# Moving the last normalisation of a fused attention layer from VectorE to GpSimd, with earlier weight splits and new scheduling keys

## The chip, the cores and the metric

The kernel runs on one core of one Trainium2 chip. The metric is device microseconds of one execution; the median of several runs is given. A profiled execution gives, beside its own time, the span from the first to the last instruction and every engine's work in it.

Short names are used throughout: PE is TensorE (the matrix engine), PEld its weight loads, DVE is VectorE, ACT is ScalarE, POOL is GpSimd, SP is SyncE, whose queue issues the DMA transfers (SPq in the profile).

## The reference

The input x has 4 batches of 512 rows and 256 columns. Each row is normalised, then two branches are computed from the normalised rows and multiplied, and x is added.

```
xn = layernorm(x)
# attention branch: 16 query heads of 128, 4 key/value groups, causal
Q, K, V = xn@Wq + bq, xn@Wk + bk, xn@Wv + bv
attn = softmax(Q K^T / sqrt(128) + causal mask)
y = gelu((attn V) @ Wo + bo)              # exact gelu
r = xn + y                                # the outer residual
s = (r - mean(r)) * rsqrt(var(r) + 1e-5) * gamma + beta
# gate branch
g = silu((silu(xn@Wgate) * (xn@Wup)) @ Wdown)   # 256 -> 1024 -> 256
out = x + s * g
```

The kernel rewrites the last two lines as out = (r - mean) * rstd * (g * gamma) + (g * beta + x).

## The kernel before

**Tiling.** Rows are handled in tiles of 128, so a batch has four tiles t = 0..3. The attention of a batch runs in four phases, one for each key/value group g, which four heads share; the 16 phases are numbered ph = 4b + g. All products in TensorE use values split in two parts (a high part rounded to the multiplier's precision and the low rest), and each product is three matmuls: high by high, high by low, low by high.

**Before the ordered part.** The first stretch of the program normalises x, transposes it, and computes the gate branch of the first three batches (`gate_up`, `down`). In its loop over b and f, `split_group` splits the query and output weights of groups 1 to 3 into two parts on POOL, using the probability tiles p1 and p2 as room, and writes the parts to device memory (`w_dram_q`, `w_dram_o`); later phases reload them. The first group is split separately. At the end of this stretch `clear` sets the edges of the probability tiles to zero (MEMSET at L273), so the edges of p1 and p2 wait until the last split's writes have landed. The multiplier, gate and shift parts g * gamma and g * beta + x go to device memory together with xn, as `fin_dram`. This stretch is ordered by the framework's scheduler.

**The ordered part.** From `order = Order(tc, nc)` on, the kernel lists tasks with an engine, an estimated cost, a key and the tasks that must come first. `Order.run` is a list scheduler that plays these through at build time: whenever an engine comes free it takes the ready task with the lowest key. The result is a fixed order of instructions on each engine; on the chip each engine runs its own list in that order, and an instruction that waits holds all behind it on its engine. `KEYS` holds 30 numbers that go into the keys, and so shape that order. The recording helper makes all of these instructions appear as L49 in the profile; they are told apart by the names of their tiles. A task's `lag` is the planner's estimate of the time from its end until others can use the result; for the loads of `fin` it is 4.0.

**A phase.** Its tasks and tile names:
- Q*, K*, V*: products for queries (into `bank`), keys (`pk`) and, once per batch, values (`pv`), then their split by ACT (high) and DVE (low) into `qT`, `kT` and `v`. `Kw` (`k0`) on POOL joins the first 128 keys again for the first scores. Values go through device memory and come back as `vr`.
- Sp, M, E, R, N: for each row tile i and subtile t the scores (`ps`, two buffers, shared with `pk` and `pv`), the mask and row minimum on DVE (`p<-ps,mask`, `least`), the exponential with its sum on ACT, the inverse of the sum on DVE, and the normalising on POOL (`p<-p,total`).
- T, H, L: transposed blocks (`u`, DVE), their high part (`pT`, ACT) and low part (`pT<-u,pT`, POOL, 1.3 us each, ten in a phase).
- W: weighted sums of values with `pT`, into the four `bank`s; then Ch and Cl (`ctxT`, ACT and DVE) and Y, the output product, into `py`.

**The outer residual.** After the fourth phase of a batch O adds the bias (DVE), G applies gelu (ACT), and for each tile: F loads `fin` (xn, g * gamma, g * beta + x) into one of two `gate` buffers, F0 adds xn (`residual`, POOL), F1 takes mean and variance (`moments2`, DVE), F2 the inverse root (`root2`, POOL), F3 `gated` and F4 `gated2` finish the tile in two DVE instructions with two tensor inputs each:

```
y = (y - mean) * fin[1]        # F3, DVE, needs F1
y = y * rstd + fin[2]          # F4, DVE, needs F2 and F3; frees the gate buffer
```

F5 stores the tile. For the first three batches this runs beside the next batch's phases; for the last it is the end of the program.

Of the kernel before, what the change touches and what calls it, by code (L numbers as in the profile page):

```python
# [14 lines left out]
ALU = mybir.AluOpType  # L15
# [4 lines left out]
EPS = 1e-5  # L20
S = 32
MASK = -1e9
KEYS = {"q0": 1.13, "q1": -0.213, "k": 1.41, "v0": 2.413, "v1": -1.03, "s0": -2.626, "s1": 0.729, "s2": -0.184, "n": -5.431, "t0": -5.662, "t1": 6.581, "t2": 4.665, "h": 0.821, "l": -0.262, "w0": -1.18, "w1": -0.794, "c": 4.145, "y0": 0.4, "y1": 1.301, "f0": 4.654, "f1": 6.182, "wo": 29.85, "wq": 0.68, "vr": 3.1, "ls": 1.3, "lt": -16.956, "lc": 5.897, "lw": 2.853, "da": 3.184, "db": 0.216}
RUNS = ((0, 1), (2, 3))
ON_ACT = (0, 1)
HIGHEST = 3.4028235e38
# [133 lines left out]
def kernel(  # L160
# [39 lines left out]
    pe, dve, act, pool, sp = nc.tensor, nc.vector, nc.scalar, nc.gpsimd, nc.sync  # L200
    latest = {}

    @contextmanager
    def behind(*keys):

        with ExitStack() as stack:
            for k in keys:
                for ins in latest[k]:
                    stack.enter_context(tc.issue_after(ins.ins))
            yield  # L210
# [23 lines left out]
    mhalf = const.tile([P, NT], F32, name="mhalf")  # L234
# [6 lines left out]
    def split_sbuf(dst, src, hi_on, lo_on):  # L241
        if hi_on is nc.scalar:
            nc.scalar.copy(dst[0], src)
        else:
            hi_on.tensor_scalar(dst[0], src, 1.0, 1.0, ALU.mult, ALU.mult)
        lo_on.tensor_tensor(dst[1], src, dst[0].bitcast(F32), ALU.subtract)
# [74 lines left out]
    rstd = const.tile([P, B, NT], F32, name="rstd")  # L321
# [33 lines left out]
    def transposed(b, t):  # L355

        if t == 0:
            xT[b] = [pair("pt", 4, f"xT_{b}_{c}") for c in range(ND)]
        xn = [normed(b, t), normed(b, t + 1)]
        pt = psum.tile([P, ND, 2, P], F32, tag="s", bufs=2, name=f"pxt_{b}_{t}")  # L360
        for c in range(ND):
            for k in range(2):
                nc.tensor.transpose(pt[:, c, k], xn[k][:, ts(c, P)], ident)
        for c in range(ND):
            dst = xT[b][c][:, :, ds(t * P, 2 * P)]
            latest["xT"] = split_psum(dst, pt[:, c].rearrange("p k q -> p (k q)"))
        if t + 2 == NT:
            for c in range(ND):
                nc.sync.dma_start(xT_dram[b][:, c], xT[b][c].bitcast(F32))

    def reload(b):
        xT[b] = [pair("xT", 2, f"xT_{b}_{c}_again") for c in range(ND)]
        for c in range(ND):
            nc.sync.dma_start(xT[b][c].bitcast(F32), xT_dram[b][:, c])
# [140 lines left out]
    def gate_up(b, f):  # L515
        gate_up_product(b, f)
        gate_silu(b, f)
        gate_times_up(b, f)
        inner_hi(b, f)
        inner_lo(b, f)  # L520
# [27 lines left out]
    def down(b, t):  # L548
        down_product(b, t)
        gate(b, t)  # L550
        gate_scaled(b, t, 0)
        gate_scaled(b, t, 1)
        gate_shifted(b, t)
        gate_out(b, t)
# [52 lines left out]
    q0, k0, vr, bank, turned = {}, {}, {}, {}, {}  # L607
# [222 lines left out]
    acc, ys = {}, {}  # L830
    mv2 = mv
# [21 lines left out]
    def activated(b, t0, t1):  # L853
        act.activation(ys[b][:, t0:t1], ys[b][:, t0:t1], AF.Gelu)

    fin, rs2 = {}, {}
# [12 lines left out]
        rs2[b, t] = rstd[:, b, t : t + 1]  # L869
        dve.tensor_scalar(rs2[b, t], mv2[:, b, t, 1:2], EPS, 1.0, ALU.add, ALU.mult)  # L870

    def root2(b, t):
        pool.tensor_tensor(rs2[b, t], rs2[b, t], mhalf[:, :1], ALU.pow)

    def gated(b, t):
        y, f = ys[b][:, t], fin[b, t]
# [24 lines left out]
    def split_group(kind, g):  # L901


        st = work.tile([P, 1024], F32, tag="stage", bufs=2, name=f"st_{kind}{g}")
        if kind == "q":
            for c in range(ND):
                nc.sync.dma_start(st[:, ts(c, 512)].rearrange("p (a n) -> p a n", a=G), wq_v[c, g])
        else:
            nc.sync.dma_start(st.rearrange("p (a n) -> p a n", a=G), wo_v[g])
        for k in range(2):  # L910
            flat = p_tiles[1 + k].rearrange("p a n -> p (a n)")
            hi, lo = flat[:, :512], flat[:, 512:1024]
            split_sbuf((hi.bitcast(F32R), lo.bitcast(F32R)), st[:, ts(k, 512)], nc.gpsimd, nc.gpsimd)
            nc.sync.dma_start(w_dram[kind, g][:, 0, ts(k, 512)], hi)
            nc.sync.dma_start(w_dram[kind, g][:, 1, ts(k, 512)], lo)

    def first_group(kind):
        views = [wq_v[c, 0] for c in range(ND)] if kind == "q" else [wo_v[0]]
        w = load_w(f"{kind}0", views)
        nc.sync.dma_start(w_dram[kind, 0], w.bitcast(F32))  # L920
        return w

    wqs[0] = first_group("q")
    wos[0] = first_group("o")

    for b in range(B - 1):
        for f in range(NI):
            gate_up(b, f)
            if b and f in (4, 5, 6):

                with behind("shifted"):
                    split_group(*(("q", 1), ("o", 1), ("q", 2), ("o", 2), ("q", 3), ("o", 3))[3 * b + f - 7])
            if b > 0 and f < NT:
                down(b - 1, f)
            if b + 1 < B:
                if f in (3, 5):
                    transposed(b + 1, f - 3)
                if b + 2 == B and f == NI - 1:
                    reload(0)
# [6 lines left out]
    pe, dve, act, pool, sp = (order.engine(e) for e in (nc.tensor, nc.vector, nc.scalar, nc.gpsimd, nc.sync))  # L946
    NPH = B * KV
    for name, n in (("s", 2), ("u", 4), ("ctx", 3), ("gate", 2), ("stage", 1)):
        order.ring(name, n)
    K = KEYS  # L950
    weights, done_w = {}, {}

    def add(name, engine, cost, key, emit, args, **kw):
        order.task((name, *args), engine, cost, key, lambda: emit(*args), **kw)
# [4 lines left out]
    def group_of(ph):  # L959
        return divmod(ph, KV)  # L960
# [8 lines left out]
    for f in range(NI):  # L969
        b, key = B - 1, -8.0 + 0.1 * f  # L970
# [8 lines left out]
    for b in (B - 2, B - 1):  # L979
        e = "POOL" if b + 1 < B else "DVE"  # L980
        c = 0.75 if b + 1 < B else 0.85
# [11 lines left out]
        for t in range(NT):  # L993
            key = base + K["db"] * t + K["da"]
            after = [("Dx", b, t), ("Da", b, t // 2), ("gb",)]
# [8 lines left out]
    for ph in range(NPH):  # L1004
        b, g = group_of(ph)
# [98 lines left out]
        for m, run in enumerate(runs):  # L1104
# [3 lines left out]
            else:  # L1108
# [8 lines left out]
                after=deps, mode=1,  # L1117
# [20 lines left out]
        if g == KV - 1:  # L1138
            late = b == B - 1
            key = ph + 1.5 + K["f0"]  # L1140
            if late:
                for t in range(NT):
                    done = [("O", b, t)] + [("E", b, g, i, u) for i, u in tiles]
                    add("G", "ACT", 0.35, key + 0.1 * t, lambda b, t: activated(b, t, t + 1), (b, t), after=done, mode=3)
            else:
                order.task(("G", b), "ACT", 3.6, key, lambda b=b: activated(b, 0, NT), after=[("O", b, t) for t in range(NT)], mode=3)
            for t in range(NT):
                k = key + (0.1 if late else K["f1"]) * t
                if late and t > 1:
                    done = [("Qp", b, g, r) for r in range(G)] + [("Kp", b, g)] + [("Vp", b, t) for t in range(NT)]  # L1150
                    add("F", "SP", 0.4, ph, load_fin, (b, t), after=done, lag=4.0)
                else:
                    done = [("O", b, 0)] if not late else [("F5", b - 1, t) for t in range(NT)]
                    add("F", "SP", 0.4, ph if late else k - 0.5, load_fin, (b, t), takes="gate", after=done, lag=4.0)
                add("F0", "POOL", 0.76, k, residual, (b, t), after=[("F", b, t), ("G", b, t) if late else ("G", b)])
                add("F1", "DVE", 0.6, k, moments2, (b, t), after=[("F0", b, t)])
                add("F2", "POOL", 0.65, k, root2, (b, t), after=[("F1", b, t)])
                add("F3", "DVE", 1.1, k, gated, (b, t), after=[("F1", b, t)])
                add("F4", "DVE", 1.1, k, gated2, (b, t), after=[("F2", b, t), ("F3", b, t)], gives=(("gate", "F", b, t),))
                add("F5", "SP", 0.4, k, stored, (b, t), after=[("F4", b, t)])  # L1160

    def idle_work(k):
# [60 lines left out]
```

## Time and profile before

| | us |
|---|---|
| median of 3 runs | 645.4 (643.51 to 647.47) |
| the profiled execution | 649.52 |
| its span | 647.7 |
| PE busy | 621.4 (96% of the span) |
| DVE busy | 433.6 (67%) |
| ACT busy | 405.7 (63%) |
| POOL busy | 444.7 (69%) |
| granted PE clock, mean over the span | 0.981 |

In the profile's rows a group reads: line, engine, operation, output<-inputs by tile names, shapes, count, busy time and mean of one, and the idle time ahead of it with what ended it. In a timeline a row begins with its start and its duration in us, xN is the number of instructions joined in it, and the square bracket gives how long the engine stood idle before it and what released it. In the windows the columns are named where they are shown.

Weighted products (W) of the batches' first groups start at 182.2, 307.2, 425.2 and 548.3 us, which places the batches in time; the last of all starts at 626.5.

### The profile page before, as it was taken

Reading aid. Unit: us, or ns where it says so; the run is one execution under the profiler, and the core shown is the slowest. Engines: PE = TensorE matmul, PEld = TensorE weight load, DVE = VectorE, ACT = ScalarE, POOL = GpSimd, SP = SyncE. Lnnn points to the kernel's source line nnn. Section 1 sums busy time; section 2 is a strip of 40 time slices with the busy share of each in tenths; the row PEclk is TensorE's granted clock in tenths of the full one; section 3 lists DMA queues with packets and bytes.
Section 4 is the critical chain, followed back from the end, with each engine's and each line's share of the span. In section 5 each row is a group of like instructions: output and inputs, shape, how many; then the busy total and the mean of one; then the engine's idle time right before and its main releaser. Section 6 shows DMA issues by size and latency. Waiting matters only on the chain.

```text
span 647.7 us, 15888 instructions
## 1 busy us (share of the span) xinstructions
PE 621.4 (96%) x6004; PEld 554.6 (86%) x6004; DVE 433.6 (67%) x1143; ACT 405.7 (63%) x1025; POOL 444.7 (69%) x577
## 2 busy tenths in 40 slices
PE   7999999799999999999999999997999999999994
PEld 6888887788989899898899989976989888898894
DVE  5973636366357676588668586878777598778545
ACT  3442426375357777598649676884587598658662
POOL 4597777286316984778678694957596687779663
PEclk8999999999998999999899999997999999999998
DMA  6867769417595568725975955195857815958701
GB/s 207 273 209 249 258 230 325 127 38 184 157 282 171 141 178 204 220 75 130 294 212 139 286 166 147 50 306 130 239 203 150 232 63 169 272 168 217 154 2 35
DMA packets 86238, 118.10 MB, mean 182 GB/s; under 512 B 5648, under 2 KB 72336, under 8 KB 82064
## 3 DMA queue, kind: packets, MB, share of 16 engines
q1 hardware_dynamic: 86160, 117.08, 62.6%
q8 instruction: 47, 0.77, 0.5%
q14 instruction: 31, 0.25, 0.1%
HBM read 87.70 MB, written 29.36 MB: 181 GB/s over the span
## 4 chain that ended last, share of the span: by engine, by line
PE 76%; DMA 8%; DVE 5%; POOL 5%; SPq 2%; ACT 2%; issue 1%; POOLq 0%; DVEq 0%
PE bank L49 30%; PE ps L49 13%; PE py L49 11%; PE pv L49 3%; DMA vr<-v_dram 3%; PE pk L49 2%; DMA w_dram_o<-p 2%; PE pd L49 2%; PE bank L229 2%; PE bank L230 2%; PE bank L231 2%; POOL pT L49 2%; POOL p L49 2%; DVE p L49 1%; DVE y L49 1%
## 5 line engine op out<-in xcount | busy, mean ns | idle before, releaser
L49 ACT ACTIVATE p<-p,least 128x32 f32<-128x32 f32 (+15 forms) x256 | 131.7, 516 | 69.4 <-DVE least L49 66.8
L49 POOL TENSOR_SCALAR p<-p,total 128x384 f32<-128x384 f32 (+7 forms) x248 | 118.9, 500 | 73.9 <-DVE total L49 68.0
L49 DVE CUSTOM_DVE_ANT_0 p<-ps,mask 128x32 f32<-128x32 f32 (+15 forms) x256 | 104.5, 431 | 70.0 <-PE ps L49 69.1
L49 PE MATMUL ps<-kT,qT 128*128 128x512 f32 (+11 forms) x576 | 116.7, 334 | 7.5 <-DVE least L49 6.8
L49 POOL TENSOR_TENSOR pT<-u,pT 128x512 fp32r<-128x512 f32 x83 | 107.4, 1305 | 23.6 <-ACT pT L49 21.8
L49 PE MATMUL bank<-pT,vr 32*128 32x128 f32 (+15 forms) x3072 | 122.3, 309 | 0.7 <-DMA vr<-v_dram 0.7
L49 PEld LDWEIGHTS bank<-pT,vr 32*128 32x128 f32 x3072 | 114.1, 186 | 8.8 <-issue 2.7
L49 PE MATMUL py<-w_o,ctxT 128*128 128x256 f32 x768 | 114.4, 289 | 0.8 <-DVE ctxT L49 0.8
L49 PEld LDWEIGHTS py<-w_o,ctxT 128*128 128x128 f32 x768 | 104.9, 192 | 4.3 <-DVE ctxT L49 1.2
L49 PEld LDWEIGHTS ps<-kT,qT 128*128 128x128 f32 x576 | 88.6, 191 | 19.2 <-DVE least L49 14.5
L49 POOL TENSOR_TENSOR pT<-u_more,pT 128x512 fp32r<-128x512 f32 x77 | 99.9, 1306 | 7.1 <-ACT pT L49 6.9
L49 PE MATMUL bank<-xT_again,w_q 128*128 128x512 f32 x384 | 95.9, 400 | 4.1 <-DVE ctxT L49 3.6
L49 PEld LDWEIGHTS bank<-xT_again,w_q 128*128 128x128 f32 x384 | 72.3, 192 | 19.4 <-DVE ctxT L49 4.3
L49 DVE STREAM_TRANSPOSE u<-p 128x512 f32<-128x512 f32 x83 | 57.9, 700 | 16.0 <-POOL p L49 14.9
L49 ACT ACTIVATE ctxT<-bank,bv_sb 128x512 fp32r<-128x512 f32 x64 | 41.9, 683 | 38.4 <-PE bank L49 33.6
L49 ACT CAST pT<-u 128x512 fp32r<-128x512 f32 x83 | 50.5, 622 | 22.7 <-DVE u L49 15.2
L49 DVE STREAM_TRANSPOSE u_more<-p 128x512 f32<-128x512 f32 x77 | 53.6, 700 | 10.8 <-POOL p L49 6.8
L49 ACT CAST pT<-u_more 128x512 fp32r<-128x512 f32 x77 | 47.5, 618 | 8.3 <-DVE u_more L49 7.2
L49 DVE SCALAR_TENSOR_TENSOR ctxT<-bank,bv_sb,ctxT 128x512 fp32r<-128x512 f32 x64 | 46.6, 738 | 8.8 <-ACT ctxT L49 8.8
L49 DVE SCALAR_TENSOR_TENSOR qT<-bank,bq_sb,qT 128x384 fp32r<-128x384 f32 x64 | 38.5, 603 | 19.4 <-ACT q L49 17.8
L49 ACT ACTIVATION_READ_ACCUMULATOR p<-p,least 128x1 f32 x256 | 48.2, 188 | 0.0
L49 ACT ACTIVATE qT<-bank,bq_sb 128x384 fp32r<-128x384 f32 x64 | 37.2, 581 | 8.6 <-PE bank L49 8.4
(133 smaller groups left out, 940.8 us busy)
## 6 DMA issues: line engine op xcount, KB each, us to landing
vr<-v_dram SPq DMA_DIRECT2D x128, 256.0 KB, 7.0
w_q<-w_dram_q SPq DMA_DIRECT2D x15, 1024.0 KB, 5.3
w_o<-w_dram_o SPq DMA_DIRECT2D x15, 1024.0 KB, 10.4
v_dram<-v SPq DMA_DIRECT2D x16, 512.0 KB, 3.6
fin<-fin_dram SPq DMA_DIRECT2D x16, 384.0 KB, 7.9
xT_dram<-xT SPq DMA_DIRECT2D x8, 512.0 KB, 5.0
fin_dram<-gate SPq DMA_DIRECT2D x16, 256.0 KB, 3.5
xT_again<-xT_dram SPq DMA_DIRECT2D x8, 512.0 KB, 4.5
```

What stands on the lines that cost most here:

```text
L49: made = getattr(self.engine, name)(*args, **kw)
L229: pe.matmul(out_ap, lhs[0], rhs[0], start=first, stop=False, **kw)
L230: pe.matmul(out_ap, lhs[0], rhs[1], start=False, stop=False, **kw)
L231: pe.matmul(out_ap, lhs[1], rhs[0], start=False, stop=last, **kw)
```

## The change

Three edits.

- **The outer residual.** In batches 0 to 2, F2 takes the roots of two tiles in one instruction (after both tiles' F1). F3 becomes `normed2`, one DVE instruction with one tensor input and two per-partition scalars, and has to wait for the root. The multiplication by fin[1] (`scaled2`, task Fg) and the sum with fin[2] (`shifted2`, F4) go to POOL as two instructions. The last batch stays as it was, with other estimated costs.
- **The splits.** Which group is split at which (b, f) is now read from a table. The order of the six splits is the same; before, three came in batch 1 (f = 4, 5, 6) and three in batch 2 (f = 4, 5, 6). Now four come in batch 1 (f = 4 to 7) and two in batch 2 (f = 4, 5).
- **The keys.** All 30 numbers in `KEYS` but none of the names change, so the order of many instructions moves a little on every engine.

```diff
-KEYS = {"q0": 1.13, "q1": -0.213, "k": 1.41, "v0": 2.413, "v1": -1.03, "s0": -2.626, "s1": 0.729, ... "f0": 4.654, "f1": 6.182, ...}
+KEYS = {"q0": 1.294, "q1": -0.162, "k": 1.154, "v0": 2.242, "v1": -0.947, "s0": -2.531, "s1": 0.181, ... "f0": 1.31, "f1": 4.659, ...}
...
-    def root2(b, t):
-        pool.tensor_tensor(rs2[b, t], rs2[b, t], mhalf[:, :1], ALU.pow)
+    def root2(b, t, n=1):
+        r = rstd[:, b, t : t + n]
+        pool.tensor_tensor(r, r, mhalf[:, :n], ALU.pow)
+
+    def normed2(b, t):
+        y = ys[b][:, t]
+        dve.tensor_scalar(y, y, mv2[:, b, t, 0:1], rs2[b, t], ALU.subtract, ALU.mult)
+
+    def scaled2(b, t):
+        y = ys[b][:, t]
+        pool.tensor_tensor(y, y, fin[b, t][:, 1], ALU.mult)
+
+    def shifted2(b, t):
+        y = ys[b][:, t]
+        pool.tensor_tensor(y, y, fin.pop((b, t))[:, 2], ALU.add)
...
+    splits = {(1, 4): ("q", 1), (1, 5): ("o", 1), (1, 6): ("q", 2), (1, 7): ("o", 2), (2, 4): ("q", 3), (2, 5): ("o", 3)}
...
-            if b and f in (4, 5, 6):
+            if (b, f) in splits:
                 with behind("shifted"):
-                    split_group(*(("q", 1), ("o", 1), ("q", 2), ("o", 2), ("q", 3), ("o", 3))[3 * b + f - 7])
+                    split_group(*splits[b, f])
...
-                add("F2", "POOL", 0.65, k, root2, (b, t), after=[("F1", b, t)])
-                add("F3", "DVE", 1.1, k, gated, (b, t), after=[("F1", b, t)])
-                add("F4", "DVE", 1.1, k, gated2, (b, t), after=[("F2", b, t), ("F3", b, t)], gives=(("gate", "F", b, t),))
+                if late:
+                    add("F2", "POOL", 0.72, k, root2, (b, t), after=[("F1", b, t)])
+                    add("F3", "DVE", 0.5, k, gated, (b, t), after=[("F1", b, t)])
+                    add("F4", "DVE", 0.5, k, gated2, (b, t), after=[("F2", b, t), ("F3", b, t)], gives=(("gate", "F", b, t),))
+                else:
+                    if t % 2:
+                        add("F2", "POOL", 0.72, k, lambda b, t: root2(b, t - 1, 2), (b, t), after=[("F1", b, t - 1), ("F1", b, t)])
+                    add("F3", "DVE", 0.4, k, normed2, (b, t), after=[("F2", b, t | 1)])
+                    add("Fg", "POOL", 0.73, k, scaled2, (b, t), after=[("F3", b, t)])
+                    add("F4", "POOL", 0.73, k, shifted2, (b, t), after=[("Fg", b, t)], gives=(("gate", "F", b, t),))
```

The whole table of keys is `q0 q1 k v0 v1 s0 s1 s2 n t0 t1 t2 h l w0 w1 c y0 y1 f0 f1 wo wq vr ls lt lc lw da db`; those of one letter or of a letter and a digit set the place of the tasks above, the last ones that of the last phase and of the late part of the gate branch.

More of the change, by code (lines that the diff above doesn't have):

```diff
@@ L22 @@
 MASK = -1e9
-KEYS = {"q0": 1.13, "q1": -0.213, "k": 1.41, "v0": 2.413, "v1": -1.03, "s0": -2.626, "s1": 0.729, "s2": -0.184, "n": -5.431, "t0": -5.662, "t1": 6.581, "t2": 4.665, "h": 0.821, "l": -0.262, "w0": -1.18, "w1": -0.794, "c": 4.145, "y0": 0.4, "y1": 1.301, "f0": 4.654, "f1": 6.182, "wo": 29.85, "wq": 0.68, "vr": 3.1, "ls": 1.3, "lt": -16.956, "lc": 5.897, "lw": 2.853, "da": 3.184, "db": 0.216}
+KEYS = {"q0": 1.294, "q1": -0.162, "k": 1.154, "v0": 2.242, "v1": -0.947, "s0": -2.531, "s1": 0.181, "s2": -0.026, "n": -5.223, "t0": -5.822, "t1": 3.68, "t2": 2.849, "h": 1.078, "l": -1.275, "w0": -1.75, "w1": -0.111, "c": 3.151, "y0": 0.375, "y1": 1.022, "f0": 1.31, "f1": 4.659, "wo": 28.733, "wq": 2.307, "vr": 3.547, "ls": 2.337, "lt": -16.381, "lc": 7.543, "lw": 2.356, "da": 2.973, "db": 1.284}
 RUNS = ((0, 1), (2, 3))
```

## The prediction

> **What bounds the kernel now.** I read the page first. TensorE is busy for 96% of the span and the next engine for 69%, and the chain that ended last is 76% PE. So what can be won or lost is PE's idle time and the time at a lower granted clock; work moved between VectorE (DVE) and GpSimd (POOL) counts only where PE waits for it.
>
> ```profile
> PE 621.4 (96%) x6004; PEld 554.6 (86%) x6004; DVE 433.6 (67%) x1143; ACT 405.7 (63%) x1025; POOL 444.7 (69%) x577
> ...
> PE 76%; DMA 8%; DVE 5%; POOL 5%; SPq 2%; ACT 2%; issue 1%; POOLq 0%; DVEq 0%
> ...
> fin<-fin_dram SPq DMA_DIRECT2D x16, 384.0 KB, 7.9
> ```
>
> Then the windows of 20 us, to find where PE is not full (columns: stretch, its length, busy time of PE, PEld, DVE, ACT and POOL, granted clock, DMA share, GB/s).
>
> ```profile
> 120.00:140.00 20.00, 16.67 (x99) 14.80 (x98) 9.17 (x29) 10.27 (x27) 10.92 (x20) 1.00 0.05 20
> ...
> 300.00:320.00 20.00, 18.80 (x241) 15.88 (x241) 14.54 (x46) 14.08 (x31) 13.15 (x23) 0.91 0.96 275
> ...
> 440.00:460.00 20.00, 16.40 (x177) 14.09 (x179) 15.28 (x30) 7.74 (x21) 13.38 (x13) 0.83 0.51 143
> ```
>
> Between 120 and 140 us PE loses 3.3 us. Between 440 and 460 it loses 3.6 us, and at clock 0.83 a further 0.17 x 20 = 3.4 us. The timelines name the causes. First, near 120 (POOL), the clearing of p-tile edges waits for the write of the last split weights to land, and the normalising of the first scores stands behind it:
>
> ```profile
> 123.24 0.15 POOL L273 MEMSET p<- 128x64 f32 x1 [3.94 <-DMA w_dram_o<-p]
> 123.38 1.25 POOL L49 TENSOR_SCALAR p<-p,total 128x32 f32<-128x32 f32 x4
> ```
>
> Second, near 440 (DVE, then POOL): the last product of the outer residual (task F4, `gated2`) sits 4.99 us in DVE while POOL runs four operations back to back, and the next DVE instruction, the `ctxT` that frees PE's bank, starts only at 445.05. The waits of PE give 3.6 us for it.
>
> ```profile
> 440.13 4.99 DVE L49 SCALAR_TENSOR_TENSOR y<-y,rstd,fin 128x256 f32<-128x256 f32 x1
> 445.05 0.74 DVE L49 SCALAR_TENSOR_TENSOR ctxT<-bank,bv_sb,ctxT 128x512 fp32r<-128x512 f32 x1
> ...
> 441.09 2.53 POOL L49 TENSOR_TENSOR pT<-u_more,pT 128x512 fp32r<-128x512 f32 x2
> 443.57 1.28 POOL L49 TENSOR_TENSOR pT<-u,pT 128x512 fp32r<-128x512 f32 x1
> ```
>
> **The base.** The profiled execution took 649.5 us (span 647.7 and 1.8 around it), 4.1 above the median of 645.4; the three runs spread from 643.5 to 647.5. About 1% is what a measurement of this kernel can tell from no change. Only 1 of 24 F3 and F4 products before the last batch took over 1.5 us, so the 440 event is probably not in every run; without it (7.2 us, below) the profile would stand at 642.3.
>
> **The moved work.** In three batches of four tiles DVE loses 12 F3 products (0.56 us mean) and 12 F4 products (14.2 us in all, the long one among them), 20.9 us, and gains 12 `normed2`, one tensor with two per-partition scalars. Its nearest row is `xn<-x,mv,rstd` and `xn<-p,mv,rstd`, the same form and size: 0.39 alone, 0.70 to 0.76 on average; 8.8 us. POOL gains 24 products and sums of 128x256 at 0.735 (`y<-y,fin`), 17.6 us, and trades 12 roots at 0.70 for six of two columns. No row has two columns; one column takes 0.70, four take 1.16, so 0.85 each: net 14.3 us more. On totals this costs nothing: POOL goes to about 72%.
>
> **Where it meets PE.**
> 1. Splits. (2,6) becomes (2,5), so the last split starts one turn earlier; a turn took POOL 4.9 us (103.16 to 108.03). In the built program, though, `k0`, which the first scores need, now stands behind the two waiting memsets, where it ran ahead of them. PE would then wait some 2.5 us earlier instead, but the chain to 125.7 starts sooner by the same landing. The inserted split in batch 1 stands between `gate` products on POOL and makes them up to 4 us later; ACT sat idle 7.4 us there with PE full, so that is hidden (0; 2 us if not). I take -3.0, bounds 0 and -3.3.
> 2. The 440 event goes with F4: 3.8 idle and 3.4 of clock, -7.2 (bounds 0 and -7.2, since another such wait can stand in).
> 3. After batch 0, the weighted products run from 307.2 to 317.2, 10.0 us, against 7.2 at 548.3: they wait 1.2 us for `vr` and then run at clock 0.57. The new keys put the values product that feeds `vr` ahead of one queries product (6 matmuls of 0.23, 1.4 us). I take -2.6, bounds 0 and -2.8.
> 4. The last scores of each batch's first group (`s1130`, `s2130`, `s3130`) move behind the weighted products, so four scores no longer run in a row into two buffers. Each run lost 0.8 us; I take half, 3 x -0.4 = -1.2.
> 5. Tail. After the last gelu (637.4) DVE alone sets the end. In the new order it takes the third tile's moments before the first F4, so the wait of 0.44 for the third root and the slowed F4 of 0.72 beside POOL are filled, and the second F4 no longer delays the third moments: -1.1 (bounds 0 and -1.5).
> 6. A new wait. On DVE the mask of that moved score now stands behind both `normed2`; these wait for the paired root, that for two residual sums on POOL, and those for `fin` to land. Middle boundary: `fin` was issued at 422.50 and took 8.49; issued 1.4 earlier it lands at 429.6. Two sums 1.5, second moments 0.8, root 0.8, two `normed2` 1.5, mask 0.6: the score's buffer is free at 434.8, with the semaphore 435.0. PE comes to the keys product that needs it at 433.2 (weighted products 424.0 to 431.2, then 0.6 and 1.4). Stall 1.8. The same sum gives 0 after batch 0, where `vr` holds PE longer, and 1.5 after batch 2: +3.3, bounds 0 and, with nothing gained on the landing, +9.
> 7. POOL's queue. The residual's sums now stand ahead of the normalising of p2. From there POOL needs 2.1+2.5+2.6+2.5+1.5+1.3+0.5+2.5 = 15.5 us to the last part of pT for the next weighted products: 432.7 + 15.5 = 448.2, against PE at 447.2. Between there and the following group POOL has 25.4 us of work and PE 24.9, so POOL is first without slack (before: 0.6 to 1.9 us). I take 1.0, 2.0 and 1.8 for the three batches, less the 3.0 us of small stalls in the same stretches (0.39, 0.54, 0.37, 0.39, 0.57, 0.73): +1.8, bounds -3 and +9.
> 8. DVE still waits for POOL in `normed2`. An `xn` beside POOL work took 0.78 to 1.38. The median lies 3.1 over 642.3; with 12 exposed instructions for 24, half of that stays: +1.5, bounds 0 and +3.
>
> [...]
>
> Sum: 649.5 - 3.0 - 7.2 - 2.6 - 1.2 - 1.1 + 3.3 + 1.8 + 1.5 = 641.0, 0.7% under the median. Its own range is 636 to 646.
>
> **Rivals.** *The waits are hidden.* Items 6 and 7 come to nothing: `fin` lands earlier, as some did (3.1 us at least). 641.0 - 3.3 - 1.8 = 635.9, 1.5% faster. For it: POOL idles 4.2 us before the residual in two of three boundaries. Against: that idle is the wait for `fin` itself.
>
> *The DVE queue holds PE (slower).* `fin` lands as late as before or later; the middle boundary decides. From a landing after 428.0 (433.2 less 5.2) each microsecond is one of PE's. At 431.0 that is 3.0, and if PE's clock halves for 6.8 us, as after 445.08, it costs 3.4 more. Three boundaries: 3 x 6.4 = 19.2 in place of 3.3 gives 656.9, 1.8% slower. For it: the landing is 7.9 in the median against the 4.0 that the order's planner reckons with. Against: the other two boundaries leave PE later, and so the stall smaller.
>
> [...] This case has both: 3.3 us idle at 122 left the clock at 1.00, but the 1.2 us at 307 were followed by 0.57.
>
> *It only shifts the waits.* Item 2 was not in the typical run, and items 6 to 8 eat the rest: 645 to 648.
>
> **How the numbers follow.** Forecast 0.45, hidden 0.25, shifted 0.13, slower 0.17. Faster by over 1% is under 638.9: the hidden case and 0.14 of the forecast's, 0.39. Slower by over 1% is over 651.9: 0.17. The rest, 0.44, is within 1%. The range, 631 to 654, takes the item bounds on the fast side, and on the other reaches to near the slower case, leaving out some 0.06 below and 0.12 above.
>
> **What would show it.** Right: no MEMSET waiting at about 123 and PE full from 120 to 140; no F3 or F4 product on DVE before the last batch; 0.3 to 1.5 us per `normed2`; PE waits of 1 to 2 us at the second keys product after batches 1 and 2, with POOL's `y<-y,fin` idle on `fin`; the end of DVE's tail about 1 us nearer the last gelu. Wrong: a PE wait over 3 us with half clock at those products, or weighted products waiting for `pT<-u` on POOL by more than 3 us per batch; or PE still idle for 3 us near 120.

## The result and the profile after

| | before | after |
|---|---|---|
| median, us | 644.59 (4 runs, 643.51 to 647.47) | 638.35 (4 runs, 637.73 to 638.92) |
| ratio, 95% interval | | 0.9874 (0.9829 to 0.9919) |
| profiled execution, us | 649.52 | 637.73 |
| span, us | 647.7 | 635.8 |
| mean granted PE clock | 0.981 | 0.994 |

1.26% faster. Timed again beside three of the kernels below, the changed kernel came to 637.3, ratio 0.9889 (0.9856 to 0.9922). The kernel before itself had medians of 644.6, 648.2, 645.2 and 648.7 in the four groups of runs, so kernels of different groups are compared by their ratios to it, not by their times. First the page of the changed kernel: busy time by engine, the chain by engine, and the median landing of `fin` (last column, us).

```profile
PE 616.7 (97%) x6004; PEld 552.4 (87%) x6004; DVE 417.6 (66%) x1131; ACT 405.0 (64%) x1025; POOL 455.7 (72%) x595
...
PE 65%; POOL 12%; DMA 9%; DVE 6%; issue 4%; ACT 2%; SPq 2%; POOLq 0%; DVEq 0%; ACTq 0%
...
fin<-fin_dram SPq DMA_DIRECT2D x16, 384.0 KB, 5.5
```

DVE went down by 16 us and POOL up by 11. PE's busy time went down by 4.7 for the same 6004 matmuls: fewer of them ran at half clock (mean clock 0.994 against 0.981), where each takes longer: in the changed kernel a 128x512 product took 0.63 to 0.78 us between 102.8 and 105, at a clock of 0.50, and 0.39 to 0.40 just before 98.7, at 1.00. POOL now has 12% of the chain, where it had 5%. The windows of the changed kernel (columns as in the prediction):

```profile
100.00:120.00 20.00, 18.41 (x94) 15.85 (x95) 11.75 (x22) 11.45 (x25) 10.06 (x16) 0.91 0.82 281
120.00:140.00 20.00, 20.00 (x131) 18.49 (x130) 11.11 (x39) 12.98 (x36) 11.50 (x20) 1.00 0.03 11
...
300.00:320.00 20.00, 19.77 (x259) 16.98 (x258) 14.68 (x41) 16.59 (x33) 12.77 (x19) 1.00 1.05 274
...
440.00:460.00 20.00, 19.82 (x275) 18.24 (x274) 13.88 (x51) 13.59 (x40) 19.45 (x28) 1.00 0.95 253
```

All three holes shown before are filled: PE is full from 120 to 140, and at 300 and 440 it is busy for 99% at full clock. POOL is busy for 97% from 440 to 460. But from 100 to 120 there is a hole that the kernel before did not have. Its cause, from the timelines of the changed kernel (POOL, ACT, PE):

```profile
90.67 0.61 POOL L245 TENSOR_SCALAR p<-st_o 128x512 fp32r<-128x512 f32 x1
91.26 0.73 POOL L543 TENSOR_TENSOR gate<-gate,x 128x256 f32<-128x256 f32 x1
...
95.56 0.39 ACT L534 ACTIVATE gate<-pd 128x256 f32<-128x256 f32 x1 [10.52 <-DMA fin_dram<-gate]
...
101.59 0.50 PE L229 MATMUL pg<-xT,w_gu 128*128 128x512 f32 x1 [2.50 <-ACT h L497]
```

The split put into batch 1 (`st_o`) stands between the gate operations of the first two tiles. The first gate's sum ends at 92.0 (89.9 before), its store lands later, ACT's third gate waits for that buffer until 95.56 (92.12 before), and PE runs dry for 2.5 us; its clock is then halved (0.50 from 102.8 to 106.2).

The timelines of three engines at the end of batch 0's last group, where the prediction expected a new wait (POOL, DVE, then PE):

```profile
308.34 0.74 POOL L49 TENSOR_TENSOR y<-y,fin 128x256 f32<-128x256 f32 x1 [5.84 <-DMA fin<-fin_dram]
...
310.93 0.71 POOL L49 TENSOR_TENSOR rstd<-rstd,mhalf 128x2 f32<-128x2 f32 x1 [0.94 <-DVE total L49]
...
311.68 1.26 DVE L49 TENSOR_SCALAR y<-y,mv,rstd 128x256 f32<-128x256 f32 x2 [0.74 <-POOL rstd L49]
312.86 0.57 DVE L49 CUSTOM_DVE_ANT_0 p<-ps,mask 128x416 f32<-128x416 f32 x1
...
312.06 3.10 PE L49 MATMUL pk<-xT_again,w_k 128*128 128x512 f32 x12
```

POOL does wait for `fin`, the mask of the moved score does stand behind both `normed2`, but the 12 matmuls of both keys products run through without a wait that the profile lists.

The places of the first weighted products (W) of each batch divide the time. `before again` is the kernel before, profiled on another occasion (644.8 us); the batches are counted from 0:

| stretch, us | before | before again | after |
|---|---|---|---|
| start to first W | 182.2 | 184.5 | 182.3 |
| first W to W of batch 1 | 125.0 | 125.0 | 121.9 |
| to W of batch 2 | 118.0 | 118.7 | 116.0 |
| to W of batch 3 | 123.1 | 115.9 | 115.8 |
| to the end of the last W | 81.0 | 80.4 | 81.4 |
| to the end of the span | 18.4 | 18.5 | 18.4 |

### The profile page after: what moved, and what is told of

Its sections match the earlier page's. It is cut to its first block, busy times and chain, and to the rows that moved or that the text cites. A ratio compares the mean times of both kernels' runs of the same rounds, so it can differ in the third digit from the quotient of the medians.

```text
span 635.8 us, 15865 instructions
## 1 busy us (share of the span) xinstructions
PE 616.7 (97%) x6004; PEld 552.4 (87%) x6004; DVE 417.6 (66%) x1131; ACT 405.0 (64%) x1025; POOL 455.7 (72%) x595
## 4 chain that ended last, share of the span: by engine, by line
PE 65%; POOL 12%; DMA 9%; DVE 6%; issue 4%; ACT 2%; SPq 2%; POOLq 0%; DVEq 0%; ACTq 0%
PE bank L49 30%; PE ps L49 13%; PE py L49 10%; POOL pT L49 4%; PE pd L49 4%; PE pv L49 3%; PE pk L49 3%; DMA vr<-v_dram 3%; POOL p L49 2%; DMA fin_dram<-gate 1%; DMA xT_dram<-xT 1%; DVE p L49 1%; DMA fin<-fin_dram 1%; POOL gate L539 1%; POOL w_d L246 1%
## 5 line engine op out<-in xcount | busy, mean ns | idle before, releaser
L49 POOL TENSOR_SCALAR p<-p,total 128x384 f32<-128x384 f32 (+7 forms) x248 | 118.7, 499 | 68.9 <-DVE total L49 68.6
L49 ACT ACTIVATE p<-p,least 128x192 f32<-128x192 f32 (+15 forms) x256 | 131.7, 516 | 56.8 <-DVE least L49 52.0
L49 DVE CUSTOM_DVE_ANT_0 p<-ps,mask 128x192 f32<-128x192 f32 (+15 forms) x256 | 104.4, 431 | 77.7 <-PE ps L49 76.5
L49 PE MATMUL bank<-pT,vr 32*128 32x128 f32 (+15 forms) x3072 | 120.7, 307 | 0.2 <-DMA vr<-v_dram 0.2
L49 PE MATMUL ps<-kT,qT 128*128 128x512 f32 (+11 forms) x576 | 115.0, 332 | 3.0 <-DVE least L49 2.4
L49 PE MATMUL py<-w_o,ctxT 128*128 128x256 f32 x768 | 112.7, 286 | 1.1 <-DVE ctxT L49 1.0
L49 PEld LDWEIGHTS py<-w_o,ctxT 128*128 128x128 f32 x768 | 103.2, 189 | 4.3 <-DVE ctxT L49 1.5
L49 PEld LDWEIGHTS ps<-kT,qT 128*128 128x128 f32 x576 | 87.0, 188 | 14.1 <-DVE least L49 8.0
L49 POOL TENSOR_TENSOR y<-y,fin 128x256 f32<-128x256 f32 x40 | 29.5, 739 | 29.7 <-ACT y L49 11.8
```

Of the source, the lines that this page charges most:

```text
L49: made = getattr(self.engine, name)(*args, **kw)
```

## Experiments

**The kernel before, once more**

> The kernel before, profiled once more on another occasion. If the 4.99 us product of the outer residual at 440 us with the half clock after it belongs to the order of the work, a VectorE product of 3 us or more and a granted clock of about 0.5 for some 7 us stand at 440 to 452 us again, and the time is 645 to 650. If it is a chance of one execution (the prediction's 'probably not in every run'), no outer product takes over 2 us there, and the profiled time is 642 to 646. In both the memset wait of 3 to 4 us near 123 us stands again, since nothing in it depends on chance.

The windows of this execution, then DVE's and POOL's timelines:

```profile
440.00:460.00 20.00, 19.66 (x271) 18.05 (x271) 15.49 (x40) 10.79 (x29) 16.52 (x21) 1.00 0.80 212
...
441.56 1.29 DVE L49 SCALAR_TENSOR_TENSOR y<-y,rstd,fin 128x256 f32<-128x256 f32 x1
...
441.27 1.30 POOL L49 TENSOR_TENSOR pT<-u,pT 128x512 fp32r<-128x512 f32 x1
442.51 2.75 POOL L49 TENSOR_TENSOR pT<-u_more,pT 128x512 fp32r<-128x512 f32 x2
```

644.8 us. The same F4 product took 1.29 us in place of 4.99, and the clock stayed at 1.00: that event was a chance of one execution. POOL had the same row of operations with two tensor inputs in its queue here, and DVE's product ended 0.28 us after the first of them. PE's wait at 123 was there (3.4 us), this time with half clock behind it (0.67 over 125 to 130 us). So the profile that the sum began with was 4.7 us longer than this one, 7.2 us of it in one stretch.

**The splits put back**

```diff
-    splits = {(1, 4): ("q", 1), (1, 5): ("o", 1), (1, 6): ("q", 2), (1, 7): ("o", 2), (2, 4): ("q", 3), (2, 5): ("o", 3)}
+    splits = {(1, 4): ("q", 1), (1, 5): ("o", 1), (1, 6): ("q", 2), (2, 4): ("o", 2), (2, 5): ("q", 3), (2, 6): ("o", 3)}
```

> The changed kernel with the table of splits of before; residual and keys stay. Theory 1, the splits net nothing: the time is 638.4 within 1.0, the wait of 3 to 4 us at 123 us is back, and the 2.5 us stall at 98.7 us with its half clock (102.8 to 106.2) is gone. Rival, the splits bring their 3 us and the stall at 98.7 us is there with either table: 641 to 642, with both stalls in the trace.

641.52 us, ratio 0.9909 (0.9877 to 0.9940). POOL and PE of this kernel:

```profile
125.12 0.15 POOL L273 MEMSET p<- 128x64 f32 x1 [4.39 <-DMA w_dram_o<-p]
...
127.59 0.66 PE L49 MATMUL ps<-kT,qT 128*128 128x288 f32 x3 [3.64 <-DVE least L49]
```

The waits moved as the theory said (3.64 back near 123, only 0.4 left at 99), but not the time: by the ratios it is 1.3 to 2.3 us over the changed kernel, between theory (within 1.0) and rival (about 3), and the intervals of the two ratios overlap. The first W stands at 182.2, 184.5, 185.4 and, in the residual-alone kernel below, 185.9 with the old table (mean 184.5), and at 182.3, 180.0, 182.9, 181.7, 182.2, 182.3 and 181.7 in seven executions with the new one (mean 181.9). At this place the splits bring 2.6 us; "they net nothing" came from comparing two executions, of which the one before was the earliest of its four.

**The residual put back** (task block of before, with its estimated costs and single roots; keys and splits new)

```diff
-                    add("F3", "DVE", 0.4, k, normed2, (b, t), after=[("F2", b, t | 1)])
-                    add("Fg", "POOL", 0.73, k, scaled2, (b, t), after=[("F3", b, t)])
-                    add("F4", "POOL", 0.73, k, shifted2, (b, t), after=[("Fg", b, t)], ...)
+                add("F3", "DVE", 1.1, k, gated, (b, t), after=[("F1", b, t)])
+                add("F4", "DVE", 1.1, k, gated2, (b, t), after=[("F2", b, t), ("F3", b, t)], ...)
```

> The changed kernel with the outer residual of before in all batches (both products on VectorE, single roots), new keys and new splits kept. Theory 1, the move of the residual brings most of the gain, because VectorE's two-input products wait for GpSimd: 643 to 646, with some products of 1.5 us or more between 430 and 620 us and PE waits behind them. Rival, the keys bring it (values and fin loads earlier, the moved scores): 638 to 640, and the stretch from the second weighted products to the third keeps its length of the changed kernel within 1 us.

657.71 us, ratio 1.016 (1.0115 to 1.0204): slower than the kernel before, which no theory expected. PE's waits, then DVE, POOL and PE near 330 us:

```profile
PE ps L49 <- DVE least L49: 16.4, 14, 2.9
```

```profile
326.25 4.29 DVE L49 SCALAR_TENSOR_TENSOR y<-y,rstd,fin 128x256 f32<-128x256 f32 x1
...
325.78 2.53 POOL L49 TENSOR_TENSOR pT<-u,pT 128x512 fp32r<-128x512 f32 x2
328.26 0.74 POOL L49 TENSOR_TENSOR y<-y,fin 128x256 f32<-128x256 f32 x1
328.95 1.30 POOL L49 TENSOR_TENSOR pT<-u_more,pT 128x512 fp32r<-128x512 f32 x1
...
339.43 0.90 PE L49 MATMUL ps<-kT,qT 128*128 128x192 f32 x6 [2.95 <-DVE least L49]
```

The wait that was chance in the kernel before now comes in each of three batches, at the same place (4.29, 4.30, 4.29 us), behind four POOL operations with two tensor inputs each. Later residual steps on DVE wait for `fin` with score masks queued behind them, and PE waits 16.4 us for masks, against 2.4 in the changed kernel. The new keys need the moved residual.

**The keys put back** (residual and splits new)

```diff
-KEYS = {"q0": 1.294, ... "f0": 1.31, "f1": 4.659, ...}
+KEYS = {"q0": 1.13, ... "f0": 4.654, "f1": 6.182, ...}
```

> The changed kernel with the keys of before; residual and splits stay. Theory 1: the keys bring the earlier values product (2.8 us after batch 0) and the earlier load of fin; without them 641 to 643, with the weighted products of 304 us at 9 to 10 us again and a PE wait of 1 to 2 us at the second keys product after batches 1 and 2. Rival, the keys bring nothing beside the residual: 637.5 to 639. Third, the longer residual chain needs the new keys and stalls without them: 646 or more.

643.37 us, ratio 0.9949 (0.9916 to 0.9982). PE, at the weighted products after batch 0:

```profile
304.48 0.83 PE L49 MATMUL ps<-kT,qT 128*128 128x416 f32 x3 [0.37 <-DVE least L49]
...
306.50 7.24 PE L49 MATMUL bank<-pT,vr 32*128 32x512 f32 x189 [0.67 <-DMA vr<-v_dram]
```

As the first theory had it for the values, W takes longer: 8.5 us here against 7.3. (In the four profiles with the old keys it takes 8.5 to 10.5, two of them partly at half clock (0.51 over 308.5 to 312 us before, 0.66 over 310 to 315 before again); in the ten with the new, 7.2 to 8.2.) Nothing waits at the second keys product, which that theory had expected. The wait of 0.37 is that of the fourth score in a row, which the new keys take away.

**The residual alone** (kernel before with the new residual block; old keys and splits)

> The kernel before with the new residual block alone: old keys, old splits. Theory 1, residual and keys pay together (keys without the moved residual were 1.6% slower than before, the moved residual and the splits without the keys 0.5% faster): the residual alone 0.3 to 0.6% faster, 641.5 to 644, no outer product over 1.5 us and weighted products after batch 0 still at 8.5 us or more. Rival, it is the residual that brings nearly all of the 1.1 to 1.3%: 637 to 640.

647.5 us, ratio 1.0005 (0.9974 to 1.0036): the moved residual alone brings nothing, less than either theory gave it. No `normed2` took over 1.39 us, so the waits on DVE are short; what it saves there is not on PE's path. Its profile has a loss that the kernel before has not. PE, within the weighted products of batch 3's second group:

```profile
579.64 0.29 PE L49 MATMUL bank<-pT,vr 32*128 32x32 f32 x5 [1.70 <-issue]
```

PE stood for 1.7 us here, and for 1.0 at the same five matmuls with the keys put back, on nothing that the profile shows ("issue"); with the keys put back the clock was 0.91 over 560 to 580 us. The stretch to the end of the last W takes 84.5 and 84.7 us in these two, against 80.4 to 81.4 in the three executions of the table. So 3.3 us of what the new keys bring in the profiles lie there; the cause of that wait is open.

The ratios in a row: residual alone 1.0005, with splits 0.9949, with keys 0.9909, with both 0.987 to 0.989; keys and splits without it 1.016. The intervals of neighbours among the first four overlap, so their order rests on the traces too. Splits alone and keys alone were not run.

**Three other places for the splits.** In the changed kernel's table, group 2's output weights moved: (2,3) for (1,7); or four splits at (1,3) to (1,6); or

```diff
-    splits = {(1, 4): ("q", 1), (1, 5): ("o", 1), (1, 6): ("q", 2), (1, 7): ("o", 2), ...}
+    splits = {(1, 2): ("q", 1), (1, 3): ("o", 1), (1, 4): ("q", 2), (1, 6): ("o", 2), ...}
```

> The changed kernel with the output weights of group 2 split after turn 3 of the third batch, between the third and the fourth tile's gate on GpSimd, one turn earlier than before and ahead of only one gate. Theory: the stall at 98.7 us goes (the first three gates stand as before) and the last split is still a turn earlier, so the wait near 123 stays away: 3 to 4.4 us less than the changed kernel. Rival, the fourth gate comes 4 us later and PE stalls for it instead, or the load of the staged weights is late and the wait near 123 comes back: the changed kernel's time or up to 2 us more.

> The changed kernel with the splits of the second batch after turns 3, 4, 5 and 6: the rounding halves of group 2's output weights stand before the first gate, the remainders between the first and second gate's products and the sums. Theory: GpSimd starts the splits one turn sooner, so the first gate's sum is done some 2 us sooner than in the changed kernel and the stall of 2.5 us shrinks to under 0.5, with its half clock gone: 3 to 4.4 us less. Rival, GpSimd waits for the staged weights to land (1.6 to 1.9 us each at 81 to 84 us in the changed kernel) and gains nothing: within 1 us of the changed kernel.

> The changed kernel with the splits of the second batch placed after turns 2, 3, 4 and 6: the output weights of group 2 then stand on GpSimd around the first tile's gate, wholly ahead of the second tile's gate. Theory, that the inserted split holds the gates back and with them ScalarE and PE at 98.7 us: since the four splits start two turns earlier, the gates are done no later than before; stall gone, and its half clock: 2.7 + 1.7 = 4.4 us less than the changed kernel, with no wait near 123. Rival, the split still stands ahead of the first gate's sum, and the stall of 2 to 3 us stays or grows: same as the changed kernel within 1 us.

| places | us | ratio, 95% interval |
|---|---|---|
| (2,3) | 642.83 | 0.9965 (0.9944 to 0.9986) |
| (1,3) to (1,6) | 637.3 | 0.9885 (0.9861 to 0.9909) |
| (1,2), (1,3), (1,4), (1,6) | 636.03 | 0.9859 (0.9833 to 0.9885) |

PE of the first, and the windows of the third:

```profile
107.65 6.30 PE L49 MATMUL bank<-xT_again,w_q 128*128 128x512 f32 x15 [5.16 <-DMA xT_again<-xT_dram]
```

```profile
80.00:100.00 20.00, 20.00 (x118) 17.56 (x117) 7.72 (x10) 6.33 (x13) 16.55 (x20) 1.00 0.71 237
100.00:120.00 20.00, 20.00 (x128) 17.98 (x127) 10.26 (x27) 10.76 (x28) 7.41 (x15) 1.00 0.69 244
```

In all three the wait at 99 us is gone, as it nearly is with the old table (0.4), so its cause is the split in front of the gates. In the first, a longer one takes its place at 102 us, for the reload of `xT_again` (neither theory had it); in the second, one of 1.8 us for the same load, so that the time comes out as the rival said, for another reason. In the third PE is full from 80 to 140 at full clock, and the first W stands at 178.2 against 180.0 to 182.9. Its median is 1.3 us under the changed kernel's, not the 4.4 of its theory, and the intervals overlap; by the trace it is the better version, 1.8 to 4.7 us ahead at the first W.

The changed kernel itself, timed beside these three:

> The changed kernel itself, timed on the same chip and in the same rounds as the three below, since 642 to 651 were seen for the kernel before from one occasion to the next. Every theory: 0.985 to 0.990 of the kernel before, the stall of 2 to 3 us at 98 to 101 us there again, because it follows from the order on GpSimd and not from chance. Were it gone in this profile, its cause would not be the inserted split.

637.3 us; the wait was there again (from 98.8 us), with 1.17 us in place of the 2 to 3 expected and no half clock behind it (1.00 from 95 to 115 us).

**Two tensors in DVE's remaining product**

```diff
-        dve.tensor_scalar(y, y, mv2[:, b, t, 0:1], rs2[b, t], ALU.subtract, ALU.mult)
+        dve.scalar_tensor_tensor(y, y, mv2[:, b, t, 0:1], fin[b, t][:, 1], ALU.subtract, ALU.mult)
...
-        pool.tensor_tensor(y, y, fin[b, t][:, 1], ALU.mult)
+        pool.tensor_scalar(y, y, rs2[b, t], None, ALU.mult)
```

> The changed kernel, in the same order on every engine, but the one product that VectorE keeps reads two tensors: (y - mean) * gamma there, and GpSimd multiplies by the root (one tensor and a per-partition scalar) in place of gamma. Rounding differs, the value computed is the same. Theory 1, a VectorE product of two tensors from on-chip memory waits for GpSimd's running operations through several of them: of the 12 products some take 1.5 to 5 us where normed2 took 0.47 to 0.70, PE waits behind them, 640 to 648. Rival, the 12 new places are harmless because GpSimd has just finished the root when they start: all under 1.0 us, 636 to 638.5.

639.7 us, ratio 0.9886 (0.9847 to 0.9925): no difference from the changed kernel. DVE and POOL of this kernel:

```profile
348.18 1.37 DVE L49 SCALAR_TENSOR_TENSOR y<-y,mv,fin 128x256 f32<-128x256 f32 x2
...
346.56 2.72 POOL L49 TENSOR_SCALAR p<-p,total 128x512 f32<-128x512 f32 x4 [0.75 <-DVE total L49]
```

The 12 products took 0.45 to 0.83 us. The rival holds: two inputs alone do not make the long wait. At the new places POOL is at its root or at one-tensor operations (`p<-p,total`); the products of over 4 us stood beside runs of four two-tensor ones on tiles of 256 or 512 columns (0.74 and about 1.3 us each).

**`fin` as if it landed later** (six multiplications of the loaded tile by one)

```diff
+        if t == 0 and b + 1 < B:
+            for _ in range(6):
+                pool.tensor_scalar(fin[b, t][:, 0], fin[b, t][:, 0], 1.0, None, ALU.mult)
         pool.tensor_tensor(y, y, fin[b, t][:, 0], ALU.add)
```

> The changed kernel, in the same order on every engine, with six multiplications of the loaded tile by one on GpSimd ahead of the first residual sum of each of three batches: estimated at 0.4 us each, 2.4 us per batch, all of it behind the landing of fin. It makes fin 'land later' without another transfer. Theory 1, the mechanism of the prediction's items 6 and 7 is right and only the landing was 1.5 us better than assumed: the moved score's mask (312.9 in the changed kernel, needed at about 313.6) comes 2.4 us later, PE waits 1.5 to 2.5 us at the second keys product at each of the three boundaries, 642 to 647 with a chance of half clock. Rival, PE or GpSimd makes it up in idle time elsewhere: 636.5 to 639, no PE wait over 1 us there.

658.97 us, ratio 1.0184 (1.0144 to 1.0225). POOL, PE, and PE's waits:

```profile
309.30 4.58 POOL L49 TENSOR_SCALAR fin<-fin 128x256 f32<-128x256 f32 x5
...
318.96 2.93 PE L49 MATMUL pk<-xT_again,w_k 128*128 128x512 f32 x6 [4.43 <-DVE least L49]
```

```profile
PE pk L49 <- DVE least L49: 13.2, 3, 4.4
```

One multiplication took 0.85 us on average, not 0.4, so the dose was 5.1 us and not 2.4. The wait came exactly at the second keys product at each of three boundaries, 4.4 us each, with half clock behind it (0.51 over 320 to 325 us, 0.59 over 440 to 445, and 0.83 over the 20 from 560). The paired root came 5.45 us later (316.38 for 310.93), and PE started 0.56 us after the second `normed2` each time. With these 0.56 us in the changed kernel, the mask is done 0.8 us before PE comes at the last two boundaries. At the first there is no room: the second keys product starts at 313.50, where the spacing of its matmuls would have it at 313.44. (There PE waited only 4.4 in the delayed run because its weighted products took 0.9 us longer.) A stretch from W to W took 7.2 us longer (123.0 for 115.8 to batch 3): 4.4 of wait and 2.8 that the halved clock and what follows account for.

**The last batch too**

```diff
                 if late:
-                    add("F3", "DVE", 0.5, k, gated, (b, t), after=[("F1", b, t)])
-                    add("F4", "DVE", 0.5, k, gated2, (b, t), after=[("F2", b, t), ("F3", b, t)], ...)
+                    add("F3", "DVE", 0.4, k, normed2, (b, t), after=[("F2", b, t)])
+                    add("Fg", "POOL", 0.73, k, scaled2, (b, t), after=[("F3", b, t)])
+                    add("F4", "POOL", 0.73, k, shifted2, (b, t), after=[("Fg", b, t)], ...)
```

> The changed kernel with the last batch's residual also on GpSimd (normed2, then two GpSimd operations of 0.73 us per tile, single roots). Theory 1, in the tail nothing else runs, so a tile's last three operations cost 0.4 + 2 x 0.73 in place of 2 x 0.48, on the path that sets the end: the tail is 1 to 2.5 us longer, 638.5 to 640. Rival, VectorE is what the tail waits for and GpSimd shares the load: 636 to 637.5.

643.49 us, ratio 0.9944 (0.9916 to 0.9973), about 0.6% over the changed kernel. DVE and POOL in the tail:

```profile
634.75 0.80 DVE L49 TENSOR_SCALAR y<-y,mv,rstd 128x256 f32<-128x256 f32 x1 [3.41 <-POOL rstd L49]
...
631.10 3.11 POOL L49 TENSOR_TENSOR y<-y,fin 128x256 f32<-128x256 f32 x4 [0.33 <-DVE y L49]
```

From the last gelu's end to the end of the work 11.25 us (628.46 to 639.71) against 6.97 (626.04 to 633.01). The loss is larger than the theory's, since a third tile's root also stands behind four products in POOL's queue while DVE idles for 3.4 us.

## Why the prediction was right, and where not

The time, 638.35, lies 2.65 under the forecast and in the forecast's own range; the direction was right and the gain just past the 1% that it gave a chance of 0.39. The rival "the waits are hidden" (635.9) came nearer in its mechanism. That the forecast came so close is in part luck: begun at the second profile of the kernel before (644.8) and without the 440 event, the same sum gives 643.5, and what brought it back is that items 6 to 8 cost next to nothing and that a stretch in no item got shorter. Item by item:

1. *Splits, -3.0.* Right in size over several executions (-2.6), wrong in the cover. "ACT idle 7.4 us" was misread as room: these 7.4 us (84.7 to 92.1) lie ahead of ACT's third gate and end with it, and that gate waits for a store, and the store for the sum on POOL that the split delays. The priced fallback, 2 us, is what it cost (1.2 to 2.5 in seven profiles, and in four of them 1.7 of clock), and the better table gets it back. In the profiled pair the stretch came out at +0.1.
2. *The 440 event, -7.2.* Right for that profile (stretch to batch 3: 123.1 to 115.8), and "probably not in every run" was right too: the second profile of the kernel before has 115.9 there. Measured against typical runs, this item is worth nothing, and the residual alone measures nothing.
3. *Weighted products after batch 0, -2.6.* Right for this pair: 10.0 to 7.3. Of that 1.2 came back with the keys (8.5); the rest is mostly the 1.7 of half clock that this place had in both profiles of the kernel before and in neither of the changed one.
4. *The moved score, -1.2.* Mechanism right, size half: the four scores take 3.91 us in a row at each of three places in four profiles with the old keys, and 2.47 for three and 0.67 for the moved one with the new, 0.8 less: -2.3.
5. *Tail, -1.1.* Right with the old keys, wrong in the changed kernel. From the end of the last W to the end of the span it is 18.4 and 18.5 us before and 17.4 in both kernels with the moved residual and the old keys, but 18.4 again with the new. There DVE's stretch from the first moments to the end did shrink, from 7.69 to 7.05. But it began 0.5 us later after the last bias sum, because ACT's table for the gelu is now loaded behind the first tile's sum instead of ahead of it, which left 0.15 (ACT, before, then keys put back, then after):

```profile
633.34 1.28 ACT L49 ACT_TABLE_LOAD   x1
```

```profile
628.87 1.28 ACT L49 ACT_TABLE_LOAD   x1
```

```profile
623.41 1.28 ACT L49 ACT_TABLE_LOAD   x1 [1.94 <-DVE y L49]
```

   The gain that the prediction looked for on DVE was taken back on an engine that it left out, ACT.
6. *The wait at the second keys product, +3.3.* The term that was mis-sized: no stall at any boundary. At the middle one the second tile's `fin` was issued 4.4 us ahead of W where the sum had 2.9, and both residual sums were done 5.6 us after W's start in place of 7.1. From there to the free buffer it took 3.5 in place of 3.9, the two `normed2` 1.25 of it in place of 1.5; and PE came 9.9 us after W's start in place of 9.2, since W itself took 7.9. So the stall of 1.8 became room of 0.8. The mechanism is shown by the delayed `fin`: place, wait, and a price of 7.2 per boundary with the clock, in the manner that the slower rival was built from (6.4). The slower case was 0 to 0.8 us away.
7. *POOL's queue, +1.8.* The 15.5 us from the paired root to the last part of pT are 15.4 (427.46 to 442.87), and the weighted products follow at 443.19 without a wait. The term was the gap to PE's arrival; nothing of it shows.
8. *DVE's waits, +1.5.* The 12 `normed2` took 0.47 to 0.70, 7.6 us against the 8.8 assumed, and none holds PE. What items 6 to 8 cost together is small: the stretch to batch 2 should have gained 3.5 by items 3 and 4 and gained 2.0 to 2.7, the one to batch 3 should have gained 0.8 and gained 0.1 over the second profile; the weighted products at the head of batches 2 and 3 take 0.5 to 0.6 us longer than in that profile. So about 1 us per batch is given back, against 6.6 in all forecast; it was not traced to one wait. The last stretch got 0.4 to 1.0 longer, in no item and not traced.

`normed2` has one tensor input and took 0.63 on average in the changed kernel (at 311.68 and 427.49 beside POOL's `p<-p,total`) against 0.39 for the same form while POOL was idle (`xn` at 22 us before), so it is slowed, though nothing waits for it; the two-input product in its place took 0.45 to 0.83, so here the number of inputs on DVE's side decided little.

One reading of rows was off: 0.56 is the mean of all 16 F3 products, and the 12 that moved took 7.1 us, so DVE lost 21.3 us of work and not 20.9. No item hangs on it.

The stretch from the first W to batch 1 (125.0 to 121.9) was in no item. It is clock alone: 3.4 us are lost to half clock between 190 and 205 in both executions before (0.77 over these 15 us in the first) and none in the one after (1.00); in the changed kernel's second profile, with 0.66 over 190 to 195, it is 123.8, and in the last batch too, with 0.72 and 0.60 over 190 to 200, 124.6. So these 3.1 us are not shown to belong to the change.

## What to carry to other kernels

Price a profile against a second one of the same kernel before costing its largest stall: here the largest stall, 7.2 of the 11.8 us by which the two profiles differ, was one execution's chance. When work is moved to another engine, ask what the order of the work can now become: the move alone was worth nothing, the new keys and splits without it cost 1.6%, and all together were worth 1.2%. When an inserted step is called hidden, follow the buffers behind it up to the engine that bounds, not the idle total of the engine between.

## What the runs showed of the hardware

- Half clock does not follow from the length of PE's wait alone. At one place, PE's wait near 99 us with the new splits, waits of 2.0, 2.3, 2.5 and 2.5 us were followed by it (0.78 to 0.80 over 100 to 105 us), and waits of 1.2, 2.3 and 2.4 were not (1.00). Elsewhere a wait of 3.3 (before) left the clock at 1.00, and seven waits of 3.4 us and more in five profiles had half clock behind them (3.6 before, 3.4 before again, 3.64 with the splits put back, 5.16 with (2,3), three of 4.4 with `fin` delayed). An episode at 0.50 lasted 3.4 us (102.8 to 106.2 after) or 6.8 (445.1 to 451.9 before), which takes 1.7 or 3.4 from a full PE; seven of the fourteen profiles show half clock between 190 and 205 us, where PE stands idle for at most 1.12 in any window of 5.
- A two-tensor product on DVE took 4.3 to 5.0 us in four cases; in the two whose POOL timeline is given (before at 440.13, residual put back at 326.25) POOL ran four two-tensor operations in a row, and the product ended 0.27 and 0.29 us after POOL fell idle. Such a row is not enough: in the second profile of the kernel before the same product took 1.29 at the head of one, 0.28 us past the end of its first operation. What decides between the two is open. Beside POOL's operations with one tensor and a per-partition scalar (`p<-p,total`) two such products took 1.37 together, and the longest of all 12 took 0.83, 0.4 more than the shortest.
- On POOL, 128x256 operations with one tensor and a scalar took 0.85 us on average (`fin<-fin`, delayed `fin`) and 0.94 (`y<-y,rstd`, two tensors on DVE), more than the sum of two tensors (`y<-y,fin`, 0.74), but 0.48 in `p<-p,total`. A root of two columns took 0.71 (0.85 on average in the kernel with the two-input product), where one of one column took 0.69 on average before.
